# Cross-attention on one core: a split key chunk undone in batch 0, wider column tiles for z, token values moved ahead, a token maximum moved back

## The chip, the cores and the metric

One Trainium2 chip, one core. The metric is the device time of one execution in microseconds (us), as the median of several runs. A profile is one execution, recorded by the hardware profiler. Its engines are PE (TensorE: matmuls, with its weight loads listed as PEld), DVE (VectorE), ACT (ScalarE), POOL (GpSimd) and SP, which issues most DMAs. Everything is computed in float32.

## The reference, cut to what matters

16 batches of 100 queries (640 wide, 8 heads of 80) attend to 718 context rows (384 wide). The last four context rows are tokens; they make a second attention over the batch's own rows, whose result is the query of a third attention over the four tokens. Both results are added, projected and added to the residual.

```
query = hidden_states @ Wq
keyt, valt = enc @ Wk, enc @ Wv                # 718 context rows
hs = _mha(query, keyt, valt)
ca_q1 = einsum('btc,th->bch', ca, Wq_ca)[:, indices, :]   # ca: the 4 tokens
ca_hs1 = _mha(ca_q1, residual, residual)       # tokens' first attention
ca_q2 = ca_hs1 @ Wq
ca_k2, ca_v2 = ca @ Wk_ca, ca @ Wv_ca
ca_hs2 = _mha(ca_q2, ca_k2, ca_v2)             # tokens' second attention
out = (hs + ca_hs2) @ Wout + b_out + residual
```

## The kernel before, in words

**Stages.** A prologue loads weights, forms the token tables and makes batch 0's keys and queries. Then a loop runs over the batches b = 0 to 15. In round b it makes the scores of batch b, the values of batch b and the keys of batch b + 1, then attention (the product a_ps, L1741) and, for whole row blocks that are finished, the output projection. The tokens' path of the next batch (class `Second`) is threaded through the same round.

**Products by sums.** Keys and values are not made block by block. The context is cut in three thirds and the 384 input columns in three, and a plan in the manner of fast matrix multiplication (`V_PLAN`, `K_PLAN`, `K4_PLAN`) does 15 products on sums of blocks (POOL makes the sums of the context, `enc_sums`, L516) instead of 18. Each entry of a plan names a PSUM bank (A to E), a product and the block of the result that the bank is then added to: by ACT's copy the first time, by a DVE addition afterwards (`Blocks.go`, L421 and L423). The next product into the same bank accumulates on it and so waits until it has been read. Keys have five column chunks of 128: four go through `Keys` (L481), the fifth is made either by `Chunk` (L761 and L751, eight steps of half-width products spread through attention) or by `last_keys` (nine full products of 240 columns, L702, no additions).

**The tokens' path.** `Second.products` makes y (L970). `take` copies its token part g on DVE (L981), `copy` the rest on ACT (L985). `scores1` makes e on POOL (four products L997, three sums L1004). `softmax1` runs the class `Maximum` in single steps: a DVE transpose (L891), a reduction quad (L893), four reductions side (L896), the reductions mx (L905), a spread of the result by ACT (`scalar`, L918) or DVE (L923), a second transpose over (L926), then the subtraction from e (L1023). How many steps run at a call is given by `softmax1(n)`; `hold` leaves the subtraction out; `fine` sets where the steps are cut. `exponentials1` is ACT's exponential of e (L1028). `softmax2` makes z: per head one product of e (100 rows) with y (33 columns), the 100 output rows cut in four column tiles `QZ` of 32, 32, 32 and 4 (L1035). The later steps use GpSimd (hs2, L1105 and L1112), with the tokens' values vb read back from `va_d` in DRAM.

**Order.** The prologue is ordered by the framework's scheduler, by priorities and modelled times; from the loop on, each engine's order is that of the program text (`manual_schedule`). Engines and DMA queues take their instructions in order. Rounds are of three kinds: `MIXED` (odd b from 3 to 13, in which the next queries are made), `PLAIN` (0, 2, 4, 10, 12, 14) and the others (1, 6, 8). `PAIRS` (after batches 2, 5, 7, 10, 12) are projected two row blocks at a time by `project_pair`, whose calls of `between` hand single steps of the tokens' maximum to DVE between reads of the output banks (L1276); the rounds after them are 3, 6, 8, 11 and 13. In PLAIN rounds both halves of attention are normalised at its end, and single steps of the maximum stand among attention's products.

**What the steps touch.** The prologue's keys of batch 0 (`Keys(0, enc).go(NF)`, nine DVE additions), the tokens' values va behind them (L1431; ACT copies them and issues two DMAs to `va_d`), the queries q_ps (L560), and the load of batch 1's context into the buffer that va's weights hold until then.

Of the kernel before, what the change touches and what calls it, by code (L numbers as in the profile page):

```python
# [14 lines left out]
B, S, H = 16, 100, 640  # L15
# [3 lines left out]
P = 128  # L19
# [18 lines left out]

PAIRS = {ENDS[r + 1]: r for r in range(0, 10, 2)}
MIXED = range(3, B - 1, 2)  # L40
PLAIN = [b for b in range(B - 1) if b not in (1, *MIXED) and b - 1 not in PAIRS]
O_AFTER = [ENDS[r | 1] if r < 2 * len(PAIRS) else ENDS[r] for r in range(len(OC))]
HT = NH * T

QC = [(0, 64), (64, S)]

QZ = [(0, 32), (32, 64), (64, 96), (96, S)]
SCALE = float(D) ** -0.5
LOW = -3.0e38

# [92 lines left out]
def kernel(  # L143
# [731 lines left out]
    class Maximum:  # L875
# [12 lines left out]
        def steps(self, top):  # L888
            name = self.name
            turned = wide(f"turned_{name}").rearrange("p (b k) -> p b k", k=32)  # L890
            yield nc.vector.transpose(turned.rearrange("p b k -> p (b k)"), top)  # L891
            quad = small.tile([P, NB], F32, tag="quad", name=f"quad_{name}")
            yield nc.vector.tensor_reduce(quad, turned, AX.X, ALU.max)  # L893
            side = small.tile([32, 4, NB], F32, tag="side", name=f"side_{name}")
            for j in range(4):
                nc.vector.tensor_reduce(  # L896
                    side[:, j, :], quad[32 * j : 32 * j + 32, :].unsqueeze(2), AX.X, ALU.max
                )
            if self.fine:
                yield  # L900
            mx = small.tile([P, NB], F32, tag="mx", name=f"mx_{name}")
            scalar = self.scalar
            rows = 64 if scalar else 32
            for lo in range(0, 64 if scalar else P, 32):
                nc.vector.tensor_reduce(  # L905
                    mx[lo : lo + 32, :],
                    side.rearrange("p q b -> p b q"),
                    AX.X,
                    ALU.max,
                )  # L910
                if self.fine and lo == 32:
                    yield
            if not (self.fine and scalar) or self.fine == "plain":
                yield
            spread = wide(f"spread_{name}").rearrange("p (b k) -> p b k", k=32)
            if scalar:
                for lo in range(0, P, rows):
                    nc.scalar.copy(  # L918
                        spread[lo : lo + rows],
                        mx[:rows].unsqueeze(2).to_broadcast([rows, NB, 32]),  # L920
                    )
            else:
# [26 lines left out]
    class Second:  # L949
# [14 lines left out]
        def products(self):  # L964

            b = self.b
            y_ps = psum1(f"y_ps_{b}")
            for c, heads in enumerate(HEADS):
                for lo, hi in QC:
                    nc.tensor.matmul(  # L970
                        y_ps[lo:hi, heads[0] * HG : (heads[-1] + 1) * HG],
                        self.xT[:, c, lo:hi],
                        m2[:, c, : len(heads)].rearrange("p h k -> p (h k)"),
                        start=(c == 0),
                        stop=(c == HC - 1),
                        skip_group_check=True,
                    )
            self.g = small.tile([S, NH, T], F32, tag="g", name=f"g_{b}")
            self.y_v = y_ps[:S, : NH * HG].rearrange("p (h k) -> p h k", h=NH)
        def take(self, lo, hi):  # L980
            return nc.vector.tensor_copy(self.g[:, lo:hi], self.y_v[:, lo:hi, :T])  # L981

        def copy(self):
            self.y = y_sbs[self.b % 2]
            nc.scalar.copy(self.y[:, :, :HT], self.y_v[:, :, T:])  # L985
            if self.b > 0:
                self.take(0, NH)

        def scores1(self, behind=None, tokens=range(T)):
# [19 lines left out]
        def softmax1(self, n=9, hold=False):  # L1009

            if not self.top:
                after = self.b - 1
                self.top = Maximum(
                    e1,
                    f"1_{self.b}",
                    after - 1 in PAIRS or after in PLAIN,
                    "plain" if after in PLAIN else after in MIXED or after - 1 in PAIRS,
                )
            if self.less:
                return  # L1020
            self.top.go(n)
            if self.top.over is not None and not hold:
                self.less = nc.vector.tensor_tensor(  # L1023
                    e1[:S], e1[:S], self.top.over[:S], ALU.subtract
                )

        def exponentials1(self):
            nc.scalar.activation(e1[:S], e1[:S], AF.Exp, scale=SCALE)  # L1028

        def softmax2(self):  # L1030
            b = self.b
            z_ps = psum1(f"z_ps_{b}")
            for h in range(NH):
                for lo, hi in QZ:
                    nc.tensor.matmul(  # L1035
                        z_ps[lo:hi, h * (HT + 1) : (h + 1) * (HT + 1)],
                        e1[:S, h * S + lo : h * S + hi],
                        self.y[:, h, :],
                        start=True,
                        stop=True,  # L1040
                    )
# [84 lines left out]
    class Last:  # L1126
# [121 lines left out]
        def project_pair(self, between):  # L1248
# [38 lines left out]
            read(b1, 1, 0)  # L1287
            nc.gpsimd.tensor_tensor(two[:, :2], two[:, 2:4], two[:, :2], less)
            nc.gpsimd.tensor_tensor(wout2[:, 0], wout2[:, 0], w(0, 0), less)
            between(2 if self.b + 1 in MIXED else 3)  # L1290
            product(b4, [(two[:, 2:4], wout2[:, 1])], True)
            product(b1, [(sum1, w(0, 1))], False)
            read(b1, 1, 1)
            product(b4, [(two[:, 4:], last(0))], False)
            read(b4, 1, 0)
            product(b2, [(two[:, 4:], last(1))], True)
            read(b2, 1, 1)
            product(b1, [(one[:, 2:4], w(1, 1)), (one[:, 4:], last(1))], False)
            read(b1, 0, 1)
            product(b3, [(two[:, :2], wout2[:, 0])], True)  # L1300
            read(b3, 1, 0)
            read(b3, 1, 1)
# [116 lines left out]
    made = second.scores1()  # L1419
    with tc.issue_after(made.ins):  # L1420
        weight_sums(nc.gpsimd, wk4)
    with tc.issue_after(masked.ins):
        keys(load_m(1))
    last_keys(0, enc)
    Keys(0, enc).go(NF)

    va = wide("va")[:, : H // 2]
    va_ps = psum("va_ps")
    for c in range(CC):
        for n in range(2):  # L1430
            nc.tensor.matmul(  # L1431
# [8 lines left out]
    for n in range(2):  # L1440
        nc.scalar.dma_start(
            out=va_d[:, n * (H // 2) : (n + 1) * (H // 2)],
            in_=va[n * B * T : (n + 1) * B * T],
        )
    with tc.issue_after(copied.ins):
        nc.vector.tensor_reduce(
            qmask, ident.rearrange("p (r u k) -> p u r k", r=RG, u=2), AX.XY, ALU.add
        )
# [14 lines left out]
    for b in range(B):  # L1463
# [38 lines left out]
        if b == 0:  # L1502
            enc_sums(enc)
            now.load(nc.gpsimd)
            now.softmax1()
            nc.scalar.copy(
                sts[0].rearrange("p a r -> p (a r)")[96:],
                low[96:].to_broadcast([P - 96, 2 * ROWS]),
            )
        st.append(scores(b, 0, tiles))  # L1510
        if b == 0:
            now.exponentials1()
# [1 line left out]
        nc.vector.tensor_tensor(most, sts[0][:, 0], sts[0][:, 1], ALU.max)  # L1514
        st.append(scores(b, 1, tiles))
        if b - 1 in PLAIN:
            now.exponentials1()
        larger(1)
        st.append(scores(b, 2, tiles))

# [9 lines left out]
        if b == 0:  # L1530
# [20 lines left out]
            exponential(1)  # L1551
            second_next, enc_next = loads()
            less = subtract(2)
            enc_next = load_rest(b + 2, enc_next)
            keys(m_next)
            now.values2(less)
            enc_sums(enc_next)
        elif b + 1 < B:
            vv = Values(b, e_in)

# [73 lines left out]
            if b == 1:  # L1634
                last.transpose()
            if last.b in PAIRS:
                last.project_pair(second.softmax1)
                if last.b == max(PAIRS):
                    nc.sync.dma_start(
                        out=forms[1],  # L1640
                        in_=wout[: 2 * P, H // 2 :].rearrange("(c p) n -> p c n", p=P),
                    )
            if not mixed and last.b in PAIRS:
                now.values2(None, later)
            if not mixed and b not in PLAIN:
                second.softmax1(8)
        else:
            room = enc_tile("spare").rearrange("p f k -> p (f k)")
# [69 lines left out]
        for g in range(2):  # L1718
# [5 lines left out]
            for n, (h, i) in enumerate(order):  # L1724
                if b in PLAIN and (g, n) in ((1, 1), (1, 8), (1, 12)):
                    second.softmax1(1)
                if b < B - 1 and (g, n) in steps:
                    chunk.go()
                    if b not in MIXED and (g, n) == steps[-1]:
                        if b in PLAIN:  # L1730
                            second.softmax1(1)
# [8 lines left out]
                for lo, hi in QC:  # L1740
# [101 lines left out]
```

## Time and profile before

| what | before |
|---|---|
| runs, us | 914.23, 911.70, 913.72 |
| median, us | 913.72 |
| profiled execution, us | 916.26 |
| its span, us | 914.5 |
| granted PE clock | 1.0 |
| instructions in the trace | 28436 |
| busy POOL / ACT / DVE, us | 706.4 / 461.9 / 720.0 |

The span is the time from the first to the last recorded instruction; the execution's own time has 1.76 us around it. In the views, a row of the timeline has start, length, engine, line, operation, output and inputs with shapes, and count; in brackets stands idle time before it and what ended it. A row by form has count, total busy us and mean ns of one, then idle time before. PE instructions are counted by hardware passes: a float32 matmul is two. A matmul's length contains its way through the array, so the pace of a series is read from the starts of its rows.

### The profile page before, as it was taken

The page shows a single profiled execution, that of the slowest core. Times are in us where ns is not written, and L with a number is a line of the kernel's source. Part 1 is how long each engine was busy: PE and PEld are TensorE (multiplying, and loading weights), DVE is VectorE, ACT ScalarE, POOL GpSimd, SP SyncE. Part 2 cuts the span into 40 slices and gives each one's busy share as a digit, 9 for nine tenths or more (in the row PEclk, how much of TensorE's full clock was granted, in tenths as well). Part 3 has the DMA queues.
Part 4 walks back from the last instruction along what each step waited for, and adds up shares of the span by engine and source line. Part 5 has one row for each costly group of instructions (what it writes and reads, how often), then busy time and mean ns, then how long its engine had stood idle before and what let it go on. Part 6 is the DMA issues. An engine that isn't in the chain of part 4 may idle for free.

```text
span 914.5 us, 28436 instructions
## 1 busy us (share of the span) xinstructions
PE 902.7 (99%) x12172; PEld 746.1 (82%) x12172; DVE 720.0 (79%) x1288; ACT 461.9 (51%) x907; POOL 706.4 (77%) x684
## 2 busy tenths in 40 slices
PE   9998999999999999999999999999999999999998
PEld 6886879888797878878788787988879888797866
DVE  2659896889848898796987869878895889848983
ACT  2334533747437473653736436364742747437441
POOL 7587999687967879697796968968797687976623
PEclk9999999999999999999999999999999999999999
DMA  8832002031300302131021301203120031310111
GB/s 257 268 96 79 30 32 85 24 106 53 96 18 27 104 24 83 54 86 51 33 75 54 105 32 47 61 25 106 54 81 32 25 106 54 91 37 24 61 46 38
DMA packets 50586, 62.99 MB, mean 69 GB/s; under 512 B 13682, under 2 KB 37810, under 8 KB 50460
## 3 DMA queue, kind: packets, MB, share of 16 engines
q1 hardware_dynamic: 48812, 59.18, 21.1%
q8 instruction: 96, 1.57, 0.7%
q10 hardware_dynamic: 1024, 1.15, 0.4%
q0 software_dynamic: 624, 0.85, 0.3%
q14 instruction: 30, 0.25, 0.1%
HBM read 55.59 MB, written 5.57 MB: 67 GB/s over the span
## 4 chain that ended last, share of the span: by engine, by line
PE 90%; DVE 4%; DMA 3%; SPq 1%; issue 0%; ACT 0%; ACTq 0%; DVEq 0%
PE s_ps L800 12%; PE a_ps L1741 11%; PE v_psA L450 11%; PE v_psB L450 9%; PE k_psA L481 8%; PE k_psB L481 7%; PE o_ps L1265 4%; PE k_psA L761 4%; PE v_psC L450 4%; PE k_psC L481 3%; PE q_ps L618 2%; PE q_ps L560 2%; PE v_psD L450 2%; PE v_psE L450 2%; PE q_psA L618 1%; DMA xT<-in_xt 1%
## 5 line engine op out<-in xcount | busy, mean ns | idle before, releaser
L997 POOL TENSOR_TENSOR e<-ca,g 100x800 f32<-100x800 f32 x64 | 98.0, 1542 | 100.2 <-ACT kT L423 76.2
L1741 PEld LDWEIGHTS a_ps<-vs,st 120*64 120x64 f32 (+3 forms) x3072 | 120.2, 124 | 10.5 <-issue 0.4
L1741 PE MATMUL a_ps<-vs,st 120*64 120x81 f32 (+3 forms) x3072 | 124.2, 233 | 0.0
L516 POOL TENSOR_TENSOR enc<-enc 128x240 f32<-128x240 f32 x144 | 111.7, 786 | 13.8 <-DMA enc<-in_enct 6.8
L1485 DVE TENSOR_TENSOR st<-st,over 120x1600 f32<-120x1600 f32 x48 | 115.2, 2401 | 0.0
L450 PE MATMUL v_psA<-wv_sb,enc 128*120 128x320 f32 x352 | 109.3, 433 | 0.0
L1112 POOL TENSOR_TENSOR hs<-hs,hs 100x640 f32<-100x640 f32 x48 | 94.8, 1975 | 3.8
L481 PE MATMUL k_psA<-enc,wk_sb 128*128 128x240 f32 x384 | 95.4, 371 | 2.1 <-DVE kT L421 1.7
L1105 POOL TENSOR_TENSOR hs<-vb,p 100x640 f32<-100x640 f32 x64 | 89.6, 1411 | 9.1 <-issue 4.8
L1004 POOL TENSOR_TENSOR e<-e,e 100x800 f32<-100x800 f32 x48 | 92.5, 1927 | 3.8
L450 PE MATMUL v_psB<-wv_sb,enc 128*120 128x320 f32 x296 | 91.8, 433 | 0.0
L481 PEld LDWEIGHTS k_psA<-enc,wk_sb 128*128 128x128 f32 x384 | 71.4, 190 | 18.6 <-POOL e L997 2.1
L450 PEld LDWEIGHTS v_psA<-wv_sb,enc 128*120 128x120 f32 x352 | 64.2, 183 | 25.0 <-DVE vs L421 0.5
L1493 ACT ACTIVATE st<-st 120x1600 f32<-120x1600 f32 x48 | 73.9, 1539 | 20.3 <-DVE st L1485 19.6
L1497 DVE TENSOR_TENSOR most<-most,st 120x800 f32<-120x800 f32 x64 | 68.3, 1068 | 14.2 <-ACT st L850 12.9
L481 PE MATMUL k_psB<-enc,wk_sb 128*128 128x240 f32 x320 | 78.0, 366 | 0.3 <-DVE sm L1087 0.3
L800 PE MATMUL s_ps<-qp,kT 64*64 64x100 f32 (+1 forms) x3072 | 73.4, 248 | 0.0
L450 PEld LDWEIGHTS v_psB<-wv_sb,enc 128*120 128x120 f32 x296 | 54.1, 183 | 21.9 <-DVE vs L421 0.4
L800 PEld LDWEIGHTS s_ps<-qp,kT 64*64 64x64 f32 (+1 forms) x3072 | 67.0, 130 | 5.6 <-issue 4.2
L1180 ACT COPY hsT<-turned_hs 32x160 f32<-32x160 f32 (+7 forms) x244 | 67.7, 278 | 3.0
L481 PEld LDWEIGHTS k_psB<-enc,wk_sb 128*128 128x128 f32 x320 | 60.6, 190 | 8.7 <-issue 0.7
L856 ACT COPY st<-s_ps 120x800 f32<-120x800 f32 x64 | 49.8, 830 | 34.3 <-PE s_ps L800 33.6
(209 smaller groups left out, 1904.2 us busy)
## 6 DMA issues: line engine op xcount, KB each, us to landing
vb<-va_d SPq DMA_DIRECT2D x62, 250.0 KB
enc<-in_enct SPq DMA_DIRECT2D x30, 240.0 KB
enc<-in_enct SPq DMA_DIRECT2D x15, 360.0 KB
xT<-in_xt SPq DMA_DIRECT2D x8, 500.0 KB
rest<-in_enct SPq DMA_DIRECT2D x31, 120.0 KB
xn<-in_x SPq DMA_DIRECT2D x11, 320.0 KB
out<-xn SPq DMA_DIRECT2D x11, 320.0 KB
ca<-in_cas SPq DMA_DIRECT2D x16, 156.2 KB
```

What stands on the lines that cost most here:

```text
L450: nc.tensor.matmul(at[0][j][:KN, : H // 2], a_form(self.enc, f)[:, j * KN : (j + 1) * KN], wv_there.get(f, wv_sb[:, W_AT[f]]), start=first ...
L481: nc.tensor.matmul(at[:, i * KT : (i + 1) * KT], wk_sb[:, W_AT[f], i], a_form(self.enc, f), start=(first and i == 0), stop=last, skip_grou ...
L516: nc.gpsimd.tensor_tensor(out, left, right, op)
L800: nc.tensor.matmul(s_ps[at][k0:k1, cols], w, rhs, start=not begun & {(at, k) for k in range(k0, k1, 32)}, stop=last, skip_group_check=True,)
L997: first = nc.gpsimd.tensor_tensor(to, self.ca[:, t, :].unsqueeze(1).to_broadcast([S, NH, S]), g[:, :, t].unsqueeze(2).to_broadcast([S, NH, ...
L1004: made = nc.gpsimd.tensor_tensor(e, e, to, ALU.add)
L1105: first = nc.gpsimd.tensor_tensor(to, self.vb[t][:S].rearrange("p (h d) -> p h d", h=NH), p2[:, :, t].unsqueeze(2).to_broadcast([S, NH, D] ...
L1112: nc.gpsimd.tensor_tensor(sums, sums, to, ALU.add)
L1485: return nc.vector.tensor_tensor(st[i], st[i], top.over[:KN].unsqueeze(1).to_broadcast([KN, 2, ROWS]), ALU.subtract,)
L1493: nc.scalar.activation(st[i], st[i], AF.Exp, scale=SCALE)
L1497: most_now = nc.vector.tensor_tensor(most[:KN], most[:KN], st[i][:, u], ALU.max)
L1741: nc.tensor.matmul(a_v[lo:hi, h % 4], st[i // 2][: KEYS[i], i % 2, h * S + lo : h * S + hi], block(i, h // 4)[: KEYS[i], h % 4], start=(i ...
```

## The change

- `QZ` goes; z is made in the two column tiles `QC`, rows 0 to 64 and 64 to 100.
- Batch 0's round is no longer PLAIN. Batch 1's fifth key chunk is made by `last_keys` ahead of attention; the third exponential comes directly behind its subtraction; batch 1's tokens' maximum takes four steps there and the rest, with subtraction and exponential, after attention's second half is issued. ACT's spread becomes a DVE copy for it.
- va is made behind the eighth key product of batch 0, in a bank of another pool.
- In PLAIN rounds the empty step of `Maximum` goes, so that ACT's spread stands one call earlier; in the rounds after them ACT's exponential of e is two instructions of half the width.
- In rounds 6 and 8 mx comes two reads later in `project_pair`, spread and the second transpose later still, and the subtraction in attention's second half.
- A constant fill of one score buffer stands earlier in the text; batch 1's `take` comes ahead of `copy`.

By engine, in the built programs: POOL's order is the same. On DVE the tokens' maximum of batch 0 (transpose, quad, side, first mx), which stood behind the nine key additions, stands behind the fifth of them, with the last four additions behind it, one mx between each. SP has the loads of batch 1's context ahead of `ca_1` and `xT_1` instead of behind them. ACT has va's copy and its two DMA issues ahead of the last three key copies.

```
-PLAIN = [b for b in range(B - 1) if b not in (1, *MIXED) and b - 1 not in PAIRS]
+PLAIN = [b for b in range(2, B - 1) if b not in MIXED and b - 1 not in PAIRS]
-QZ = [(0, 32), (32, 64), (64, 96), (96, S)]
...
-            if not (self.fine and scalar) or self.fine == "plain":
+            if not (self.fine and scalar):
                 yield
...
-        def exponentials1(self):
-            nc.scalar.activation(e1[:S], e1[:S], AF.Exp, scale=SCALE)
+        def exponentials1(self, parts=1):
+            w = ROWS // parts
+            for lo in range(0, ROWS, w):
+                part = e1[:S, lo : lo + w]
+                nc.scalar.activation(part, part, AF.Exp, scale=SCALE)
...
             for h in range(NH):
-                for lo, hi in QZ:
+                for lo, hi in QC:
                     nc.tensor.matmul(
                         z_ps[lo:hi, h * (HT + 1) : (h + 1) * (HT + 1)],
...
-            between(2 if self.b + 1 in MIXED else 3)
+            between(2)
...
             read(b4, 1, 0)
+            if self.b + 1 not in MIXED:
+                between(2)
...
             read(b1, 0, 1)
+            if self.b + 1 not in MIXED:
+                between(1)
...
     last_keys(0, enc)
-    Keys(0, enc).go(NF)
-
+    first_keys = Keys(0, enc)
+    first_keys.go(8)
     va = wide("va")[:, : H // 2]
-    va_ps = psum("va_ps")
+    va_ps = bank("va_ps")
+    turn[0] += 1
...
+    first_keys.go(NF)
...
         if b - 1 in PLAIN:
-            now.exponentials1()
+            now.exponentials1(2)
...
             less = subtract(2)
+            exponential(2)
+            last_keys(b + 1, enc)
             enc_next = load_rest(b + 2, enc_next)
...
             enc_sums(enc_next)
+            second.softmax1(4)
...
-                last.project_pair(second.softmax1)
+                last.project_pair(lambda n: second.softmax1(n, True))
...
-            if not mixed and b not in PLAIN:
+            if b == 1:
                 second.softmax1(8)
...
-        if b < B - 1 and not b in MIXED:
+        if 0 < b < B - 1 and b not in MIXED:
             chunk = Chunk(b + 1, enc)
             chunk.go(2)
...
-                if b < B - 1 and (g, n) in steps:
+                if 0 < b < B - 1 and (g, n) in steps:
                     chunk.go()
+                    if b - 1 in PAIRS and b not in MIXED and (g, n) == (1, 6):
+                        second.softmax1()
...
+            if b == 0 and g == 1:
+                second.softmax1()
+                second.exponentials1()
```

More of the change, by code (lines that the diff above doesn't have):

```diff
@@ L979, in products @@
             self.y_v = y_ps[:S, : NH * HG].rearrange("p (h k) -> p h k", h=NH)
+            if b == 1:
+                self.take(0, NH)
         def take(self, lo, hi):
@@ L985, in copy @@
             nc.scalar.copy(self.y[:, :, :HT], self.y_v[:, :, T:])
-            if self.b > 0:
+            if self.b > 1:
                 self.take(0, NH)
@@ L1016, in softmax1 @@
                     after - 1 in PAIRS or after in PLAIN,
-                    "plain" if after in PLAIN else after in MIXED or after - 1 in PAIRS,
+                    after in (*MIXED, *PLAIN) or after - 1 in PAIRS,
                 )
@@ L1421 @@
         weight_sums(nc.gpsimd, wk4)
+        nc.scalar.copy(
+            sts[0].rearrange("p a r -> p (a r)")[96:],
+            low[96:].to_broadcast([P - 96, 2 * ROWS]),
+        )
     with tc.issue_after(masked.ins):
@@ L1505 @@
             now.softmax1()
[L1506 to L1509, printed above, removed]
         st.append(scores(b, 0, tiles))
@@ L1644 @@
                 now.values2(None, later)
-            if not mixed and b not in PLAIN:
+            if b == 1:
                 second.softmax1(8)
```

## The prediction

> **What bounds the kernel now.** I read the page first: busy shares, then the chain that ended last.
>
> ```profile
> PE 902.7 (99%) x12172; PEld 746.1 (82%) x12172; DVE 720.0 (79%) x1288; ACT 461.9 (51%) x907; POOL 706.4 (77%) x684
> ...
> PE 90%; DVE 4%; DMA 3%; SPq 1%; issue 0%; ACT 0%; ACTq 0%; DVEq 0%
> ```
>
> TensorE (PE) is busy for nearly all of the 914.5 us span and makes 90% of the chain. So two things are worth time: what lengthens or shortens PE's own work, and where PE waits. The second is small and has few rows. The view of waits, PE alone, has as its longest entries (total, times, longest):
>
> ```profile
> PE k_psA L481 <- DVE kT L421: 1.7, 1, 1.7
> ...
> PE k_psA L761 <- DVE kT L751: 0.9, 2, 0.5
> PE k_psA L761 <- DVE kT L421: 0.9, 1, 0.9
> PE o_ps L1265 <- DVE xn L1276: 0.7, 2, 0.3
> ```
>
> The third entry is batch 0's split key chunk, the second and fourth are batches 6 and 8, and these three the change attacks. PE's idle time in all is 914.5 - 902.7 = 11.8 us; a change that gives PE more than that to do cannot win by them.
>
> **The change part by part.** Sums are made against the profiled execution, 916.26 us (span 914.5 and 1.76 around it). The median of the runs shown is 913.72, 2.54 lower; I add the same difference to it at the end.
>
> **1. The product z in two column tiles.** Per batch, 8 heads x 4 tiles x 2 matmul instructions (64) become 8 x 2 x 2 (32), each pair loading 64 and 36 weight columns instead of 32, 32, 32 and 4. The moving side stays at 33 columns. By form (count, then total us and mean ns of one), and from PE's timeline:
>
> ```profile
> L1035 PE MATMUL z_ps<-y_sb,e 100*32 100x33 f32 x768 | 12.3, 198 | 0.0
> ...
> L1347 PE MATMUL k_ps<-tokens,wk_sb 128*64 128x64 f32 x60 | 2.0, 224 | 0.0
> ```
>
> ```profile
> L1035 PEld LDWEIGHTS z_ps<-y_sb,e 100*32 100x32 f32 x768 | 10.4, 109 | 4.2 <-issue 2.5 <-ACT e L1028 1.7
> ...
> L1347 PEld LDWEIGHTS k_ps<-tokens,wk_sb 128*64 128x64 f32 x60 | 1.8, 138 | 0.4 <-issue 0.4
> ```
>
> ```profile
> 18.71 1.97 PE L1347 MATMUL k_ps<-tokens,wk_sb 128*64 128x64 f32 x60
> ...
> 66.14 0.75 PE L1035 MATMUL z_ps<-y_sb,e 100*32 100x33 f32 x64
> ...
> 311.61 1.86 PE L1741 MATMUL a_ps<-vs,st 120*64 120x81 f32 x48
> 313.30 0.37 PE L761 MATMUL k_psA<-enc,w_sums 128*64 128x240 f32 x1
> ```
>
> z now takes 0.75 us for 16 groups of four; less the 0.20 tail of the last one that is 34 ns a group. A load of 64 columns lasts 138 ns against 109 for 32: 0.9 ns more per column. Hidden or not, that is what must be fed in before the next group can start in the same tile. The row nearest to the new form is k_ps, pairs of 64-column tiles with a short moving side: (1.97 - 0.22) / 30 pairs = 58 ns a pair. Attention's pairs (48 instructions, 24 pairs, from 311.61 to 313.30) take 70 ns for 81 moving columns, 0.87 ns a column; for 33 columns that would be 29 ns, so k_ps at 64 columns (56 by this rate) is only just beyond its stream, and whether its 58 ns is load or stream is the question. I take it as load, since the loads show a cost per column and the stream of 33 columns could not hide 64. Then z costs 16 x (58 - 34) = 0.38 us more per batch. Batch 0's z lies ahead of the 1.7 us wait of the first entry above and vanishes in it; the other 15 lie on PE's path: **+5.7 us**. Bounds: at the pace of the stream, 16 x (29 - 34) x 15 = -1.2; with load and stream one after the other, 58 + 29 = 87 ns, 16 x 53 x 15 = +12.7.
>
> **2. Tokens' values among batch 0's keys.** Six matmuls (va) move from behind the last key product to behind the eighth of fifteen, with the ACT copy and its two DMA issues ahead of two key copies on ACT. SP's loads of batch 1's context, which wait until va has read its input, come sooner and now stand ahead of the ca and xT loads. All of this alone is free: PE does the same work in another order. But the built program shows a second move. On DVE, the tokens' maximum for batch 0 (L891 on) stood behind all nine key additions; now its transpose, reductions and first mx stand after the fifth, with four additions behind them. The transpose waits for GpSimd's e. The rows, POOL, DVE and PE in turn:
>
> ```profile
> 38.63 3.04 POOL L997 TENSOR_TENSOR e<-ca,g 100x800 f32<-100x800 f32 x2 [6.53 <-DVE g L981]
> ...
> 48.91 1.88 POOL L1004 TENSOR_TENSOR e<-e,e 100x800 f32<-100x800 f32 x1
> ```
>
> ```profile
> 45.90 0.66 DVE L421 TENSOR_TENSOR kT<-k_psC,kT 128x480 f32<-128x480 f32 x1 [1.85 <-ACT kT L423]
> ...
> 50.82 1.01 DVE L891 STREAM_TRANSPOSE turned<-e 128x800 f32<-128x800 f32 x1 [2.02 <-POOL e L1004]
> 51.86 0.99 DVE L893 TENSOR_REDUCE quad<-turned 128x25 f32<-128x800 f32 x1
> 52.89 0.71 DVE L896 TENSOR_REDUCE side<-quad 32x25 f32<-32x25 f32 x4
> 53.63 1.29 DVE L905 TENSOR_REDUCE mx<-side 32x25 f32<-32x100 f32 x4
> ```
>
> ```profile
> 42.27 0.97 PE L481 MATMUL k_psB<-enc,wk_sb 128*128 128x240 f32 x4
> 43.08 0.97 PE L481 MATMUL k_psA<-enc,wk_sb 128*128 128x240 f32 x4
> ...
> 47.94 0.97 PE L481 MATMUL k_psA<-enc,wk_sb 128*128 128x240 f32 x4
> 48.84 1.83 PE L1431 MATMUL va_ps<-wvca,tokens 128*64 128x320 f32 x12
> 50.61 1.62 PE L560 MATMUL q_ps<-xT,wq_sb 128*128 128x200 f32 x8
> ```
>
> POOL's order and inputs are unchanged, so e still ends at 50.79 (48.91 + 1.88). The addition that ran at 45.90 can start only after the transpose, quad, side and one mx: 53.63 + 0.32 (a quarter of 1.29) = 53.95, and ends at 54.63. The second product into bank C waits for it, as its semaphore says: it overwrites what that addition reads. PE meanwhile: va from 43.17 to 44.94 (48.84 to 50.61 is 1.77), then five key products of 0.81 (42.27 to 43.08) to 49.0, then nothing until 54.7. Bank C's product ends at 55.5; the last product waits for the next addition (mx 0.32 and 0.66 more, 55.63) and ends at 56.5; the query products start at 56.6 instead of 50.61: **+6.0 us**. POOL has nothing there that could be late next, and what follows, scores and the first DVE chain, hangs on the queries and moves along. Bounds: 0 if DVE does not meet the wait, 7 if all four additions had to be done first.
>
> **3. Batch 0's fifth key chunk in full products** (for batch 1). PE, from the first split product to the next scores:
>
> ```profile
> 89.14 0.43 PE L761 MATMUL k_psC<-enc,w_sums 128*64 128x120 f32 x4
> 90.42 0.63 PE L761 MATMUL k_psA<-enc,w_sums 128*64 128x240 f32 x4 [0.85 <-DVE kT L421]
> ...
> 100.45 0.92 PE L970 MATMUL y_ps<-m,xT 128*64 128x72 f32 x20
> 101.30 1.43 PE L800 MATMUL s_ps<-qp,kT 64*64 64x100 f32 x56
> ```
>
> That is 12.16 us. After: 9 full products, 18 instructions at 0.81/4 each, 3.65; attention's 192 instructions at 1.69/48 each, 6.76; y 0.85; two changes of shape at 0.09 each (48.84 - 47.94 - 0.81, above): 11.44. So **-0.7 us**. The eight DVE additions go; the maximum's spread comes to DVE (0.99) from ACT, beside attention, where DVE has 6.8 us for some 8 operations of 1 us or less. Bounds -1.0 (the wait alone) to +0.3 (nothing of the wait saved).
>
> **4. The maximum later beside output, batches 6 and 8.** PE, then DVE:
>
> ```profile
> 411.97 1.24 PE L1265 MATMUL o_ps<-wout_sb,hsT 128*128 128x320 f32 x4
> 413.55 1.85 PE L1265 MATMUL o_ps<-wout_sb,hsT 128*128 128x320 f32 x6 [0.34 <-DVE xn L1276]
> ...
> 418.75 1.02 PE L1741 MATMUL a_ps<-vs,st 119*64 119x81 f32 x24
> 420.22 0.63 PE L761 MATMUL k_psA<-enc,w_sums 128*64 128x240 f32 x4 [0.45 <-DVE kT L751]
> ```
>
> ```profile
> 412.24 0.65 DVE L905 TENSOR_REDUCE mx<-side 32x25 f32<-32x100 f32 x2
> ...
> 418.36 1.36 DVE L1023 TENSOR_TENSOR e<-e,over 100x800 f32<-100x800 f32 x1
> ```
>
> Four output instructions take 1.08 (0.27 each) but 1.58 pass: 0.50 lost, because mx (0.65) stood ahead of the read; now mx stands two reads later. 24 attention instructions take 0.85 but 1.47 pass: 0.62 lost behind the subtraction (1.36), which now comes in attention's second half. 1.1 us per batch, **-2.2 us** for two. Late next would be ACT's spread, which follows mx and moves back with it; only the new second transpose and the last two reads hang on it, and PE does not. Bounds -2.2 to 0.
>
> **5. The rest at 0**: the exponential in two halves and ACT's earlier spread (batches 2, 4, 10, 12, 14) shorten only what PE's list of waits does not show; the 1.7 us of load idle behind ACT e in the row of L1035 is the most it could give. ACT is at 51%, so two shorter activations have room.
>
> Sum: 5.7 + 6.0 - 0.7 - 2.2 = +8.8: 925.1 for a profiled execution, **922.5** beside the median.
>
> **The rivals.**
> - *The clock drops in the stop.* PE's first matmuls ran at half pace, as these two rows, the same four instructions, show:
>
> ```profile
> 4.84 2.63 PE L391 MATMUL v_ps<-wv_sb,enc 128*120 128x320 f32 x4
> ...
> 7.85 1.24 PE L391 MATMUL v_ps<-wv_sb,enc 128*120 128x320 f32 x4
> ```
>
> If 5.7 us without matmuls sets PE back to that, 6 us at half pace, which is about the time from the span's start to full pace, cost up to 3.0 more: 925.5. No stop in this trace is long enough to tell. The Trainium skill (TensorE: Matmul & The Clock Gate, "HAM oscillation — how this bites in real kernels") speaks for it: it lets PE idle for about 3.4 us before the clock halves. Chance 0.24.
> - *Load and stream of one tile do not overlap*: +12.7 in place of +5.7, 929.5. The k_ps row speaks against it (58 ns, not 114). The skill's page, in its section "The mechanism", would have it: loads overlap running matmuls only in other row groups, and these tiles share theirs. 0.04.
> - *e is there when DVE comes to it*: stop 0, the rest as forecast: 916.5. Against it stands 50.82, where DVE waited for e in the old order too. 0.12.
> - *z at the pace of the stream*: -1.2 in place of +5.7, 915.6, if weight loads stay hidden at any width. For it: k_ps exceeds its stream by 2 ns only. 0.12.
> - *Faster, by the same mechanism*: with z at the stream's pace everything but the stop sums to -4.1, so it decides by when e ends: the change gains if PE's stop is under 4.1 us, e before about 48.9, and without a stop gives 909.6. 0.06.
>
> **How the numbers follow.** Forecast 0.42. A measurement of this kernel tells about 0.3% (2.7 us, 911.0 to 916.5) from no change. Slower: forecast, clock, no overlap and half of "no stop" (on the boundary), 0.42 + 0.24 + 0.04 + 0.06 = 0.76; within: 0.06 + 0.12 = 0.18; faster 0.06. The range takes the forecast, the clock and both cases of one sign cheaper: 915.3 to 926.5 holds 0.9; a higher low end would cut two cases that differ by 1 us.
>
> **What would show it.** A gap of 5 to 6 us on PE at 49 us, with DVE's transpose first and key additions after 54 us; none means step 2 is wrong. z over 1.0 us per batch for 32 instructions; 0.7 or less means step 1 is wrong. Batches 6 and 8 without waits for xn and for L751. Matmuls at half pace behind the gap mean the clock. The forecast fails if e comes earlier or z's loads stay hidden.

## The result and the profile after

| | before | after |
|---|---|---|
| median, us | 913.59 (5 runs, 911.35 to 914.23) | 923.04 (5 runs, 921.53 to 924.36) |
| ratio, 95% interval | 1 | 1.0111 (1.0092 to 1.0130) |
| profiled execution, us | 916.26 | 923.04 |
| its span, us | 914.5 | 920.6 |
| mean granted clock | 1.0 | 0.996 |

The change costs 9.45 us by the medians; 922.5 had been forecast. From here on every time stands beside the runs of before on the same chip, whose median was 914.01 for e1 to e4, 914.08 for e5 to e8 and 914.33 for e9 to e12.

The page of the changed kernel, busy shares and the chain that ended last:

```profile
PE 908.6 (99%) x11646; PEld 754.2 (82%) x11646; DVE 719.0 (78%) x1283; ACT 458.9 (50%) x906; POOL 705.0 (77%) x684
...
PE 90%; POOL 4%; DMA 2%; DVE 1%; SPq 1%; issue 1%; ACT 0%; ACTq 0%; POOLq 0%
```

PE has 526 instructions fewer and is busy 5.9 us longer; its idle time is 12.0 us (920.6 - 908.6) as against 11.8. Fewer instructions and more time is what step 1 expects of z; a part of the busy time is work at half the clock, below. That the idle time is the same hides an exchange, which the waits of PE show (total, times, longest):

```profile
PE k_psC L479 <- DVE kT L419: 5.3, 1, 5.3
```

One new wait of 5.3 us stands where before had smaller ones: batch 0's 1.7 and 0.9, those of batches 6 and 8, and 1.1 for a DMA in the prologue. Now the place of the stop, PE's rows:

```profile
47.20 0.97 PE L479 MATMUL k_psB<-enc,wk_sb 128*128 128x240 f32 x4
53.43 1.97 PE L479 MATMUL k_psC<-enc,wk_sb 128*128 128x240 f32 x4 [5.25 <-DVE kT L419]
55.19 1.81 PE L479 MATMUL k_psA<-enc,wk_sb 128*128 128x240 f32 x4
56.79 9.36 PE L558 MATMUL q_ps<-xT,wq_sb 128*128 128x200 f32 x50
66.08 1.60 PE L798 MATMUL s_ps<-qp,kT 64*64 64x100 f32 x64
```

DVE's rows of the same stretch say why:

```profile
49.69 1.01 DVE L889 STREAM_TRANSPOSE turned<-e 128x800 f32<-128x800 f32 x1 [6.77 <-POOL e L1004]
...
52.50 0.31 DVE L903 TENSOR_REDUCE mx<-side 32x25 f32<-32x100 f32 x1
52.74 0.64 DVE L419 TENSOR_TENSOR kT<-k_psC,kT 128x480 f32<-128x480 f32 x1
...
53.75 0.66 DVE L419 TENSOR_TENSOR kT<-k_psA,kT 128x480 f32<-128x480 f32 x1
```

DVE stood 6.77 us on the transpose, which waited for POOL's e, with four key additions behind it; the addition that frees bank C ended at 53.38 and PE went on at 53.43. And the clock, in windows of 2 us (window, length, PE busy and instructions, granted clock, DMA share, GB/s):

```profile
48.00:50.00 2.00, 0.17 (x1) 1.00 0.94 297
50.00:52.00 2.00, 0.00 (x0) 0.86 0.76 270
52.00:54.00 2.00, 0.57 (x2) 0.50 0.03 12
...
56.00:58.00 2.00, 2.00 (x7) 0.50 0.00 0
58.00:60.00 2.00, 2.00 (x12) 0.93 0.00 0
```

PE came back at half pace: the four instructions of bank C passed in 1.76 us (53.43 to 55.19) instead of 0.81. So the rival "the clock drops in the stop" has happened, beside everything that the forecast named.

z by form (count, total us, mean ns) is what step 1 expected:

```profile
L1038 PE MATMUL z_ps<-y_sb,e 100*64 100x33 f32 x256 | 17.9, 224 | 0.0
L1038 PE MATMUL z_ps<-y_sb,e 100*36 100x33 f32 x256 | 15.6, 208 | 0.0
```

```profile
L1038 PEld LDWEIGHTS z_ps<-y_sb,e 100*64 100x64 f32 x256 | 16.1, 138 | 3.9 <-issue 3.9
```

32 instructions a batch, 64-column loads of 138 ns as in k_ps. From z's first row to the next shape PE takes 1.05 us a batch (0.93 in batch 0); before mostly took 0.68.

What did not fit was batch 0: from its z to batch 1's z there passed 38.81 us instead of 42.31, 3.5 less where the sum had 0.7. The two profiles could not say whether that came from the earlier context, from the full products or from the one execution of before. That, the price of z, the stop and the clock were the questions for the experiments.

### The profile page after: what moved, and what is told of

It is laid out like the page before. It is cut to its first block, busy times and chain, and to the rows that moved or that the text cites. A ratio compares the mean times of both kernels' runs of the same rounds, so it can differ in the third digit from the quotient of the medians.

```text
span 920.6 us, 27374 instructions
## 1 busy us (share of the span) xinstructions
PE 908.6 (99%) x11646; PEld 754.2 (82%) x11646; DVE 719.0 (78%) x1283; ACT 458.9 (50%) x906; POOL 705.0 (77%) x684
## 4 chain that ended last, share of the span: by engine, by line
PE 90%; POOL 4%; DMA 2%; DVE 1%; SPq 1%; issue 1%; ACT 0%; ACTq 0%; POOLq 0%
PE a_ps L1756 12%; PE s_ps L798 12%; PE v_psA L448 10%; PE v_psB L448 8%; PE k_psA L479 8%; PE k_psB L479 6%; PE o_ps L1268 5%; PE k_psA L759 4%; PE v_psC L448 3%; PE k_psC L479 3%; PE q_ps L616 2%; PE q_ps L558 2%; PE z_ps L1038 2%; PE v_psD L448 2%; PE v_psE L448 2%; PE q_psA L616 1%
## 5 line engine op out<-in xcount | busy, mean ns | idle before, releaser
L514 POOL TENSOR_TENSOR enc<-enc 128x240 f32<-128x240 f32 x144 | 108.9, 766 | 10.7 <-DMA enc<-in_enct 3.6
L1499 DVE TENSOR_TENSOR st<-st,over 120x1600 f32<-120x1600 f32 x48 | 111.4, 2322 | 0.0
L1115 POOL TENSOR_TENSOR hs<-hs,hs 100x640 f32<-100x640 f32 x48 | 97.8, 2037 | 3.8
L1511 DVE TENSOR_TENSOR most<-most,st 120x800 f32<-120x800 f32 x64 | 65.6, 1025 | 13.7 <-ACT st L848 12.5
L798 PE MATMUL s_ps<-qp,kT 64*56 64x100 f32 (+1 forms) x3072 | 73.1, 248 | 0.0
L798 PEld LDWEIGHTS s_ps<-qp,kT 64*56 64x56 f32 (+1 forms) x3072 | 66.9, 130 | 5.4 <-issue 4.2
```

The costliest lines, as they stand in the source:

```text
L514: nc.gpsimd.tensor_tensor(out, left, right, op)
L798: nc.tensor.matmul(s_ps[at][k0:k1, cols], w, rhs, start=not begun & {(at, k) for k in range(k0, k1, 32)}, stop=last, skip_group_check=True,)
L1115: nc.gpsimd.tensor_tensor(sums, sums, to, ALU.add)
L1499: return nc.vector.tensor_tensor(st[i], st[i], top.over[:KN].unsqueeze(1).to_broadcast([KN, 2, ROWS]), ALU.subtract,)
```

## The experiments

Theory A and theory B in the expectations differ in what they make of that extra gain in batch 0: A puts it down to the context that is loaded earlier, B to the full products.

**e1: z alone, on the kernel before.**

```
-                for lo, hi in QZ:
+                for lo, hi in QC:
```

> The kernel before with z in two column tiles and nothing else. Theory (step 1: a group of four or two instructions is paced by the columns that are loaded): z takes 1.05 us a batch instead of 0.68, batch 0's disappears in the 1.7 us wait, 15 x 0.37 = +5.6 us, about 919.2 beside 913.6. Rival (the longer z is hidden by waits that follow it): z rows as long, time within 1 us of before.

Measured 917.95, ratio 1.0046 (1.0029 to 1.0064): +3.9 by the medians. z takes 1.05 us in batches 1 to 15, as expected; the sum is 1.7 smaller than 5.6, though the interval (2.7 to 5.8 us) still holds 5.6. A part of it, 0.8 us, comes from the four-tile form, below (e5). The profile of e1 also lacks the 1.7 us wait that before's has in batch 0; whether that makes up the rest was not measured.

**e2: values ahead alone, on the kernel before.**

```
-    Keys(0, enc).go(NF)
+    first_keys = Keys(0, enc)
+    first_keys.go(8)
...
-    va_ps = psum("va_ps")
+    va_ps = bank("va_ps")
+    turn[0] += 1
...
+    first_keys.go(NF)
```

> The kernel before with the tokens' values among batch 0's keys and nothing else; DVE's order in the built program is the one of the changed kernel (transpose behind the fifth key addition). Both theories: a stop of 5 to 6 us on PE and half the clock for some 6 us behind it, +7.9 at the start. Theory A (the gain of 2.8 us in batch 0 that was not forecast comes from batch 1's context, which is loaded earlier): it shows here as well, +5.1, about 918.7. Theory B (it comes from the fifth chunk's full products and what moves with them): +7.9, about 921.5.

Measured 920.42, ratio 1.0072 (1.0055 to 1.0088): +6.4, between the two. The stop, with the half clock behind it, makes more than half of the change's cost. PE's rows, and the clock in two windows:

```profile
53.77 1.97 PE L481 MATMUL k_psC<-enc,wk_sb 128*128 128x240 f32 x4 [5.23 <-DVE kT L421]
...
56.88 8.62 PE L560 MATMUL q_ps<-xT,wq_sb 128*128 128x200 f32 x50
65.43 0.81 PE L800 MATMUL s_ps<-qp,kT 64*64 64x100 f32 x26
```

```profile
53.00:54.00 1.00, 0.23 (x1) 0.60 0.00 0
...
56.00:58.00 2.00, 2.00 (x11) 0.85 0.00 0
```

The same stop, but from 53.77 to the scores 11.66 us pass instead of 12.65. If the clock is either 1.00 or 0.50, these means put the half clock of e2 from 53.2 to 56.6 us, and those of the changed kernel put it there from 51.4 to 58.3. So it was over when e2's queries began (8.55 us for them, 9.29 in the changed kernel). What half the clock costs differs by a microsecond between these two executions.

**e3: z back in four tiles; e4: values back behind the keys; e5: both**, each on the changed kernel.

```
 e3:
+QZ = [(0, 32), (32, 64), (64, 96), (96, S)]
...
-                for lo, hi in QC:
+                for lo, hi in QZ:
```

```
 e4:
-    first_keys.go(8)
+    first_keys.go(NF)
...
-    va_ps = bank("va_ps")
-    turn[0] += 1
+    va_ps = psum("va_ps")
...
-    first_keys.go(NF)
```

> The changed kernel with z back in four column tiles. Theory (step 1): 15 x 0.37 = 5.6 us less than the changed kernel, about 917.4 (+3.8 on before); the stop at 47 to 53 us and the half clock stay. Rival (the wider tiles also save something elsewhere, as half the instructions): over 918.5.

> The changed kernel with the tokens' values back behind batch 0's keys; DVE's order there is the one of before. Both theories: stop and half clock go. Theory A (batch 0's extra gain of 2.8 us hangs on the earlier context): it goes too, 7.9 - 2.8 = 5.1 us less than the changed kernel, about 917.9. Theory B (it hangs on the full products): all 7.9 us come back, about 915.1, and from batch 0's z to batch 1's z stay 38.8 us.

> The changed kernel with z in four column tiles and the tokens' values behind the keys, so that the fifth chunk of batch 0, the later maximum in batches 6 and 8 and the small edits are left. Theory A (extra gain from the earlier context): -0.7 - 2.4 - 0.3, about 910.2 beside 913.6. Theory B (extra gain from the full products): 2.8 less, about 907.4. Rival to both (the parts left over gain nothing by themselves): 913.6.

Measured: e3 917.32, 1.0041 (1.0027 to 1.0054); e4 915.94, 1.0020 (1.0005 to 1.0034); e5 910.61, 0.9968 (0.9955 to 0.9982). What is left of the change without z and va is a gain of 3.5 us. By the medians z costs 5.7 (after against e3) and 5.3 (e4 against e5), the early values 7.1 (after against e4) and 6.7 (e3 against e5); with each median taken against its own runs of before, 6.1 and 5.4, 7.5 and 6.8. e4 lies by theory B and e5 by theory A, so neither explains batch 0. Its rows do. In e1 and e4 the first z rows of batches 0 and 1 are:

```profile
64.24 1.06 PE L1035 MATMUL z_ps<-y_sb,e 100*64 100x33 f32 x31
...
104.35 1.12 PE L1035 MATMUL z_ps<-y_sb,e 100*64 100x33 f32 x32
```

```profile
66.01 1.06 PE L1038 MATMUL z_ps<-y_sb,e 100*64 100x33 f32 x31
...
104.82 1.12 PE L1038 MATMUL z_ps<-y_sb,e 100*64 100x33 f32 x32
```

40.11 us without the full products (e1, values behind) and 38.81 with them (e4, values behind too): 1.3 us go with step 3, as e4 has the full products and e1 the split ones. Then 42.31 in before's profile had 2.2 more than e1, and e5 has 41.15, 2.3 more than e4, though in neither pair the context comes earlier. In both slow ones DVE's pair of "larger" (L1497, L1509) and POOL's first products of batch 1 run at the same time. Before, DVE and POOL:

```profile
69.22 4.97 DVE L1497 TENSOR_TENSOR most<-most,st 120x800 f32<-120x800 f32 x2
70.29 3.04 POOL L997 TENSOR_TENSOR e<-ca,g 100x800 f32<-100x800 f32 x2
```

and after, again DVE and POOL, where DVE starts first:

```profile
75.13 3.23 DVE L1511 TENSOR_TENSOR most<-most,st 120x800 f32<-120x800 f32 x2
75.34 4.41 POOL L997 TENSOR_TENSOR e<-ca,g 100x800 f32<-100x800 f32 x2 [11.40 <-ACT st L854]
```

The pair lasts 4.97 us where POOL's two products get in, and POOL's products last 4.41 instead of 3.04 where DVE gets in; the second order is the one without the wait of PE. That gave a third theory, tried in e9.

e5 also shows that z in four tiles often takes more than 0.68 us. PE's rows of batch 10:

```profile
597.42 0.53 PE L1039 MATMUL z_ps<-y_sb,e 100*32 100x33 f32 x36
598.42 0.42 PE L1039 MATMUL z_ps<-y_sb,e 100*32 100x33 f32 x28 [0.46 <-issue]
```

In the middle of z PE stands, waiting for nothing that the profile shows, and this z takes 1.34 us. Added over the 16 batches the time above 0.68 is 0.4 us in the profile of before and 0.3 to 1.6 in the six others with four tiles (e2, e3, e5, e6, e9, e10), 0.8 in the mean of the seven. None of the 80 z in two tiles (after, e1, e4, e7, e11) takes more than 1.05 us.

**e6: values early, DVE's order of before, z in four tiles.** Besides e3's edit, the transpose of batch 0's tokens' maximum is held until the last key addition:

```
-            yield nc.vector.transpose(turned.rearrange("p b k -> p (b k)"), top)
+            self.first = nc.vector.transpose(turned.rearrange("p b k -> p (b k)"), top)
+            yield
...
             now.softmax1()
+            wait_for(now.top.first, first_keys.moved)
```

> The changed kernel with z in four column tiles, the tokens' values early as in it, and the transpose of batch 0's tokens' maximum held on DVE until the last key addition, so that the additions have the order of before. Step 2's reason (the stop comes from DVE's order alone): no stop, no half clock, about 907.4 by theory A and by theory B. Rival (early values stop PE in another way, by ACT's copy or the bank): a wait of over 1 us remains among batch 0's keys, over 909.

Measured 909.08, 0.9955 (0.9939 to 0.9971). PE has no wait among batch 0's keys. So the stop came from DVE's order and not from the early values, which cost nothing that shows: e5, with late values, took 910.61, and e9, below, 908.12.

**e7 and e11: the stop kept, PE kept at work.** Products of the identity into an unused bank, ahead of the waiting key product; e11 also keeps the last key addition in its place on DVE.

```
+    first_keys.go(5)
+    for _ in range(18):
+        nc.tensor.matmul(va_both[:, 1, :P], ident, ident, start=True, stop=True)
     first_keys.go(NF)
...
 e11 only:
+            wait_for(now.top.spread, first_keys.moved)
```

> The changed kernel with 18 idle 128-column products on PE ahead of the key product that waits (about 3.9 us of the 5.4 us stop). They add nothing to the path if the wait ends when it did. Clock theory: PE's rows behind the stop run at full pace, 1.9 us less than the changed kernel, about 921.1. Rival (the half pace there comes from something else, a port or the DMA): rows at half pace still, 923.0.

> The kernel of e7 (18 idle products in the stop) with DVE's spread held until the last key addition, since in e7 that addition slid behind three other operations and PE waited 1.12 us for it among the query products. Clock theory: from the waiting key product to the first scores 10.8 us instead of 12.65 in the changed kernel, all rows at full pace, 1.9 us less than the changed kernel, about 921.1. Rival (half pace from something else): 12.6 us.

Measured: e7 921.43, 1.0081 (1.0069 to 1.0094); e11 919.51, 1.0059 (1.0045 to 1.0073). PE of e7, then of e11:

```profile
48.34 4.18 PE L1460 MATMUL va_ps<-ident 128*128 128x128 f32 x36
53.74 1.08 PE L479 MATMUL k_psC<-enc,wk_sb 128*128 128x240 f32 x4 [1.23 <-DVE kT L419]
...
60.36 5.34 PE L558 MATMUL q_ps<-xT,wq_sb 128*128 128x200 f32 x30 [1.12 <-DVE kT L419]
```

```profile
52.95 1.08 PE L479 MATMUL k_psC<-enc,wk_sb 128*128 128x240 f32 x4 [1.24 <-DVE kT L419]
...
63.45 1.60 PE L798 MATMUL s_ps<-qp,kT 64*64 64x100 f32 x64
```

The bank waits as long as before, but PE's rows behind it run at full pace: 10.50 us from bank C to the scores in e11 (52.95 to 63.45), 12.65 in the changed kernel, so the clock cost 2.15 there, and 1.16 in e2. The medians differ by 3.5; 0.5 us of the rest lies at the start of the profiled executions and 0.66 in one later batch (65.35 against 64.69 us from z to z), and it is not claimed for the clock. In e7 most of the gain went into another wait, 1.12 us, because the last key addition had slid behind three DVE operations.

**e8: z in three column tiles** of other widths.

```
+QZ3 = [(0, 32), (32, 64), (64, S)], [(0, 64), (64, 96), (96, S)]
...
-                for lo, hi in QC:
+                for lo, hi in QZ3[b % 2]:
```

> The changed kernel with z in three column tiles: 32, 32 and 36 columns in even batches, 64, 32 and 4 in odd ones, to tell what paces z. By the columns loaded into the widest tile (about 0.9 ns each in a row): even 0.68 to 0.73 us from z's first row to the next shape, odd 1.05 us. By the number of instructions (48 for 64 took 0.68): 0.51 in both. By the sum of the columns: the same time in both.

One execution, 962.65 us: all three expectations failed. z of batch 1 and its window:

```profile
115.53 3.36 PE L1039 MATMUL z_ps<-y_sb,e 100*64 100x33 f32 x48
...
115.60:118.80 3.20, 3.20 (x48) 1.00 0.02 5
```

z takes about 3.29 us in odd batches and 2.97 in even ones, without idle time, and in the one shown at the full clock. Within a head of an odd batch the starts lie 79, 154, 6, 30, 16 and 127 ns apart: the long steps, 154 and 127, stand where tiles of 64 columns and of 32 follow each other. The Trainium skill (TensorEngine Tiling (Array Packing), "Key Properties") has a rule for it, that a change of the tiling mode drains TensorE; this trace agrees, with 3.29 us for 16 rounds of 64, 32 and 4 columns as against 1.05 for 16 of 64 and 36, but the experiment could not answer what it was made for. e12 does.

**e9 and e10: POOL's first product behind DVE's pair**, on e5 and on e6.

```
-            second.scores1()
+            second.scores1(seen)
             m_next = load_m(b + 2)
```

> The kernel of e5 (z in four tiles, values behind the keys) with one wait more: POOL's first score product for batch 1 waits for DVE's last 'larger' of batch 0, as it does in all later batches. Theory (the 1.7 and 0.34 us waits of PE in batch 0 come from POOL's product getting ahead of that DVE pair, which then takes 4.97 us instead of 2.4): the DVE pair takes about 2.4, both waits go, batch 0's z to batch 1's z takes 38.6 to 39.0 us instead of 41.15, and the median falls by up to 2.3 us against e5, to 908.3 to 910. Rival (the wait comes from something else, or POOL's product is then late for batch 1's maximum): 41 us still, or a new wait of like size behind it, 910.6 or more.

> The kernel of e6 (z in four tiles, values early, DVE's order of before) with the same wait on POOL. In e6 the DVE pair took 3.23 us and PE did not wait. Theory: 0.85 us off DVE's chain, nothing off PE: within 0.5 us of e6 (909.1). Rival: POOL's product becomes late and PE waits at the fifth chunk or at batch 1's z, 1 us or more slower.

Measured: e9 908.12, 0.9937 (0.9922 to 0.9951), against e5's 910.61; e10 909.27, 0.9951 (0.9935 to 0.9968), against e6's 909.08. First e5, DVE, POOL and PE, then e9, DVE and POOL:

```profile
67.77 4.97 DVE L1509 TENSOR_TENSOR most<-most,st 120x800 f32<-120x800 f32 x2
68.84 3.04 POOL L998 TENSOR_TENSOR e<-ca,g 100x800 f32<-100x800 f32 x2
77.06 1.05 PE L480 MATMUL k_psA<-enc,wk_sb 128*128 128x240 f32 x4 [1.62 <-DVE kT L420]
```

```profile
67.73 2.01 DVE L1509 TENSOR_TENSOR most<-most,st 120x800 f32<-120x800 f32 x2
69.97 3.04 POOL L998 TENSOR_TENSOR e<-ca,g 100x800 f32<-100x800 f32 x2 [1.18 <-DVE most L1509]
```

4.97 us become 2.01, by 2.96, about what POOL's two products take (3.04); batch 0's z to batch 1's z falls from 41.15 to 38.56, and PE waits nowhere in it. So the 1.7 us wait in the prediction's second fence, which I had read as part of the kernel, came from POOL and DVE taking turns. The Trainium skill (SBUF — State Buffer, "SBUF: two separate sides") states it as an exclusive lock: a DVE operation with two SBUF inputs and a GpSimd operation that reads SBUF block each other for a whole instruction, and the first to start goes first. The traces agree in both directions, with the 4.97 and 4.41 us above.

e9 has the lowest median of the study, 6.2 us under before; e6 and e10, 5.0 and 5.1 under it, differ from e9 by no more than their intervals.

**e12: small products by themselves.** Ten series of 24 groups in the place of e7's idle products, as in:

```
+    for k in range(24):
+        for lo, hi in [(0, 36), (64, S)]:
+            nc.tensor.matmul(spare_ps[lo:hi, :33], ident[:S, lo:hi], ident[:S, :33], start=True, stop=True)
```

> The changed kernel with ten series of 24 groups of small products put into the stop, written to an unused part of a bank, to measure what paces z: 100 rows, moving 33 columns unless said. In this order: column tiles 32+32+32+4; 32+32+32+32; 64+36; 36 (at 0) + 36 (at 64); 64+64; 64+36 with 66 moving; 64+64 with 81 moving; one tile of 100; 32+32; one tile of 64. Load theory (the widest tile's columns must be fed in before the tile can go on): per pass of a group 34 to 42, 34 to 42, 65, 36 to 40, 65, 65, 70, 100 and more, 34 to 42 and 65 ns. By the sum of the columns loaded: 65 for 100, 83 for 128, 47 for 72, 65, 83, 65, 42 and 42. By a fixed cost of a pair of 64-wide tiles: 65 for every pair of these, whatever it loads.

One execution (957.52 us; the series account for most of what it is longer). Rows from PE's timeline, from the series 64+36 on:

```profile
59.81 5.22 PE L1468 MATMUL va_ps<-ident 100*64 100x33 f32 x95
64.75 0.33 PE L1471 MATMUL va_ps<-ident 100*36 100x33 f32 x2
...
67.82 2.96 PE L1474 MATMUL va_ps<-ident 100*64 100x33 f32 x95
...
76.91 4.42 PE L1483 MATMUL va_ps<-ident 100*100 100x33 f32 x48
81.26 2.74 PE L1486 MATMUL va_ps<-ident 100*32 100x33 f32 x96
83.93 5.33 PE L1489 MATMUL va_ps<-ident 100*64 100x33 f32 x48
```

```profile
62.00:64.70 2.70, 2.70 (x56) 0.50 0.03 10
...
66.00:67.70 1.70, 1.70 (x65) 0.50 0.35 137
...
69.00:70.50 1.50, 1.50 (x58) 1.00 0.00 0
...
79.00:81.20 2.20, 2.20 (x27) 1.00 0.00 0
...
84.00:89.00 5.00, 5.00 (x48) 0.50 0.00 0
```

The windows are needed because the clock changes between the series. At half the clock: 64+36 takes (64.75 - 59.81) / 48 = 103 ns a pass, 36+36 takes (67.82 - 64.75) / 48 = 64 with its start and 60 in between, one tile of 64 takes 107. At the full clock: 64+64 takes (2.96 - 0.2) / 47 = 59, one tile of 100 (81.26 - 76.91) / 48 = 91. So a pair of 64-wide tiles has no fixed price (60 against 103 in the same state), the sum of the columns doesn't count (64+64 at 59 is what 64+36 takes in z), and a single tile pays its columns and nothing for the stream of 33 beside them. Two more series at the full clock moved more columns: 64+36 with 66 moving took 58 to 59 ns a pass (70.57 to 73.37 us), 64+64 with 81 moving 71 to 73 (73.39 to 76.91). The load theory holds for these forms: the widest tile's columns at about 0.9 ns each set the pace, unless more columns are moved than loaded. The first two series, tiles of 32 and 4 columns, were interrupted by stops of PE and give no pace.

## Why the prediction was right, and where it was not

The number was right, 922.5 for 923.04, and so were the mechanism and the place of both large terms; one cost that the forecast left out was made up for by terms that came out a little lower than it had them. By its steps:

1. **z, forecast +5.7: right, mis-sized by little.** z's rows grew by 0.371 us (0.38 forecast) for the reason given, as e12 shows by itself: loaded columns, not stream. The term came to about 5.0 (15 x 0.37 = 5.6, a bit of batch 0, less 0.8 for what the four-tile form takes above 0.68); 3.9, 5.7 and 5.3 were measured. That batch 0's z vanishes in the 1.7 us wait was wrong in its reason: e9 shows that the wait was no fixed one.
2. **Values ahead, forecast +6.0: right, the cost of the clock left out.** The stop was 5.3 us where 5.7 stood, in the row where it was forecast, and e6 shows that DVE's order makes it. The step that failed is the choice to count the matmuls behind the stop at full pace: the rival "the clock drops in the stop", at a chance of 0.24, is what happened. Its price was 2.15 (e11 beside after), 1.16 in e2, and not the upper bound of 3.0. From the first key product to the scores PE took 30.02 us after (36.06 to 66.08) and 22.06 before (37.20 to 59.26), 7.96 more; less the clock's 2.15 the stop cost 5.8.
   The clock fell after 50 us, with PE's last product ended by 48.2, while e7 and e11, which left PE idle for 1.2 us, stayed at 1.00. The mean of 0.86 in the window from 50 to 52 puts the fall at about 51.4, some 3.3 us after PE's last product; in e2 and e3 it came 4.7 and 5.2 us after it (48.5 to 53.2 and 48.0 to 53.1). The Trainium skill (TensorE: Matmul & The Clock Gate, "HAM oscillation — how this bites in real kernels") has about 3.4 us of idleness for it; the traces agree in so far as stops of 5.2 us brought the fall and 1.2 us did not, but they show no fixed delay. The half clock then lasted 6.8 us in the changed kernel and 3.4 in e2 and e3. In the traces every stretch between two changes of the granted clock is a whole multiple of 3.41 us (3.41, 6.83, 13.65, 44.37, 47.79), so the half clock comes in steps, and the price of one and the same stop with it; what sets the start of these steps is not shown.
3. **Batch 0's fifth chunk, forecast -0.7: right in sign, too small.** -1.3 (e1 to e4) and -1.1 (e2 to e3: 39.74 to 38.63). The wait that goes was 0.85 in the profile of before and 1.4 and 1.3 in e1 and e2: where nothing delays PE earlier in the batch, it comes to the split products sooner and waits longer. The sum had missed that, as it took the 1.7 and the 0.85 as independent.
4. **Maximum later in batches 6 and 8, forecast -2.2: right.** These rounds went from 58.03 to 56.85 us (e1 to e4, z to z, both alike), -2.4 for the two, and no waits for xn or for the split keys remain in the list of after.
5. **The rest at 0**: about -0.3, 0.06 a batch in four batches (47.22 to 47.16).

Sum of the terms as found: 5.0 + 5.8 + 2.15 - 1.2 - 2.4 - 0.3 = +9.05, against +8.8 forecast and +9.45 measured (8.4 to 11.9 by the interval). The right sum is thus partly luck: the clock's 2.15 is about what the other terms fell short together, 1.9. The two profiles differ by 6.8 only; the profiled execution of before had the POOL and DVE collision (2.3 us) and started its keys 1.1 us later than after. How many of before's runs have the collision was not measured; that their times spread over 5.2 us (910.84 to 916.04), and those of e9 over 1.8, would fit.

Of the rivals, "no stop" and "z at the stream's pace" are refuted by the rows, and so is the case on the faster side, which hung on both. "Load and stream don't overlap" is refuted by e12's single tiles, 91 ns for 100 columns and not 28 more, which the stream of 33 columns would add by the 0.87 ns of attention's columns; so the rule that the prediction names beside that rival does not hold for these tiles.

## What to carry to other kernels

Where a scheduler orders an engine, look at the order that a moved block leaves on the engines that it doesn't touch: here the six moved matmuls cost nothing, and the four key additions that came to stand behind a waiting transpose cost about 7 us. A stop on PE of 5 us, as here, is to be priced with the half-speed matmuls behind it; after one of 1.2 us there were none. A wait in a profile may itself be a collision of two engines in that one execution; before it is used as cover for other work, ask what would make it go away.

## What had not been expected of the hardware

- PE can stand still in a series of short instructions. e12's first series, four tiles of 32 and 4, made 184 instructions in 1.75 us and then stood with nothing that the profile names:

```profile
48.69 1.75 PE L1462 MATMUL va_ps<-ident 100*32 100x33 f32 x184
55.21 0.32 PE L1462 MATMUL va_ps<-ident 100*32 100x33 f32 x7 [4.78 <-issue]
```

  The second series, again four tiles of 32 columns, stopped once more, for 1.47 us. The stops in z in four tiles, which took up to 0.66 us, look like the same thing. That instructions are not supplied fast enough is argued, not shown.
- Mixed tile sizes in one series (e8) cost about 3 us for 48 instructions, against 1.05 for 32 of one size.
- The clock can fall while PE's rows show no idle time. In e12 it fell to 0.50 again at about 81.5 us, though PE had worked without a stop since 59; the series there load few columns or use one tile at a time. In e8 it fell for 3.4 us at 76.1, 226.3 and 683.7 us, each time as a z of mixed tiles ended (73.2 to 76.1, 223.1 to 226.4 and 680.0 to 683.3). Idle time as the profile counts it is therefore not the whole condition; what is stays open.
